# Single images at the end of a filter phase, and constants, loads and table writes moved in a hand-ordered Trainium2 kernel

## The chip, the cores and the metric

The kernel runs on one core of a Trainium2 chip. The core has a matrix engine (TensorE, PE in the profile, with PEld for its weight loads), a vector engine (VectorE, DVE), a scalar engine (ScalarE, ACT), GpSimd (POOL) and a sync engine (SyncE, SP) that mostly issues DMA transfers. All work from on-chip memory, and the products of TensorE land in PSUM banks of 128 partitions by 512 float32. Everything here is float32.

The metric is the device time of one execution in microseconds (us). A profile is one further execution under the hardware profiler; its span runs from the first to the last instruction.

## The reference, cut to what matters

Eight images of 128 channels by 32×32 pixels go through two layers. The first has attention over the 1024 pixels of an image and then a spectral transform unit (STU), the second a deformable convolution of three taps and eight experts of which two are used per pixel.

```python
# layer 0
x = x + attention(ln_c(x))                  # left as it is by the change
t = tokens(x)                               # (8, 1024, 128)
t = t + stu(ln_t(t))
# layer 1
x = image(t)
x = x + deform_conv(ln_c(x))
t = tokens(x)
t = t + experts(ln_t(t))

def stu(u):      # only one of four fractions (1, 1/2, 1/4, 1/8) of the tokens has weight 1
    U_plus[t, k]  = sum_s phi[s, k] * u[t - s]             # 16 causal filters
    U_minus[t, k] = the same with alternating signs
    return sum_k sigma[k]**.25 * (U_plus[:, k] @ Mpp[k] + U_minus[:, k] @ Mpm[k]) \
           + sum_{i<3} shift(u, i) @ Mu[i]

def deform_conv(x):   # per pixel and tap j: position = base + offset(x)
    for j in range(3):
        s = bilinear sample of x at (y, xc)                # four neighbours
        out += sigmoid(mask(x))[j] * s @ conv_w[j].T

def experts(x):       # softmax over 8, the two largest, renormalized
    return sum over the two of p * (x @ expert_w[e] + expert_b[e])
```

The fractions enter the kernel as spans of tokens: each span of an image has its own sum of the weighted matrices.

## The kernel before

**Attention.** `attention_bounded` works until about 1020 us and stores each image of the first sublayer to a DRAM buffer `x1d`. The change doesn't touch it.

**What stands between.** After a branch (line 1258), `mix_weights` works out the softmax weights of the fractions, `Spectral.__init__` builds its constants (among them `mu`, the matrices of the three lags, from four loads of `M_u` through one buffer), and `DeformAndExperts.__init__` builds the second layer's constants with some 45 small DMAs from SP. All of that is issued before the first image is prepared.

**The filter phase.** `spectral_and_second_layer` writes the order of all engines' instructions out by hand: each engine executes its instructions in the order in which this function emits them. `GROUPS` puts the images into four pairs. A group passes 16 filters, so there are 64 iterations. An iteration has four parts (parity of the token, term plus or minus), and in each part, for each image of the pair, `filter_image`: four accumulating matmuls of 512, 384, 256 and 128 columns into one of two PSUM banks (`pu`, line 1154), copied out by ACT into `us` (line 1158). Between them stand the products of the iteration before with the mixing matrices `mf` (`mix`, line 1142): per part, spans of 64, 64 and 128 tokens behind the first image and one of 256 behind the second, each over both images of the group. The first mix of a group is preceded by `start_sums`, the lags. After a group's last mix `finish` copies the sums `po` to `x2`.

`load(n + 2)`, at the end of iteration n, loads the next but one filter (`teto`, lines 1049 and 1052, three buffers) and its matrices (`mf`, three buffers). The first group builds the matrices and stores them to DRAM, later groups load them (line 1064). All of these go through SP.

**The second layer beside the filters.** `layer.image` is a generator of some 96 steps. It turns the image back to tokens, normalizes and turns again; makes eight products with the convolution weights (`p_g`, line 856), copied by ACT to `gs` (line 859); writes them as a table of four shifted slots to DRAM with 24 writes of 256 KB from SP (line 864), twelve after the fourth product and twelve after the eighth; works out positions and weights (`corners`); fetches with 24 indirect DMAs from POOL (line 894, nine buffers) and accumulates with 96 DVE operations (line 909); normalizes (`tt`), turns (`p_turn`, line 772), computes the gates (`p_l`, line 971), and applies the experts with sixteen matmuls (`p_e`, line 927) through two PSUM banks and 64 DVE operations (line 933). It ends with `p_out` (lines 944, 947) and the store.

From the second iteration of a group on, `behind` holds the two images of the group before and `spec.prepare` of the next group. After each unit of an iteration (eight units, one for each part and image) `todo` grows by `RATE`, 1.8, and as many whole steps of `behind` run. Each step's TensorE instructions therefore stand in TensorE's order between filter products, and TensorE waits there if their inputs are late.

**The tail.** Images 6 and 7 have no filters left to stand beside. They run after the last `finish`, the second one 50 steps behind the first.

Of the kernel before, what the change touches and what calls it, by code (L numbers as in the profile page):

```python
# [32 lines left out]
GROUPS = ((0, 1), (2, 3), (4, 5), (6, 7))  # L33
RATE = 1.8
STAGGER = 50
# [637 lines left out]
class DeformAndExperts:  # L673
# [4 lines left out]
    def __init__(  # L678
# [3 lines left out]
        nc = self.nc = tc.nc  # L682
        cp = ctx.enter_context(tc.tile_pool(name="d_const", bufs=1))
        self.sb = ctx.enter_context(tc.tile_pool(name="d_sb", bufs=2))
        self.ps = ctx.enter_context(tc.tile_pool(name="d_ps", bufs=banks, space=PSUM))
        self.ident, self.dram, self.out = ident, dram, out

# [8 lines left out]
        with nc.allow_non_contiguous_dma(reason="small weights"):  # L696
            for tap in range(TAPS):
                at = TAPS * C + 9 * tap
                for xy in range(2):
                    nc.sync.dma_start(  # L700
                        self.gw[:, at + 3 * xy : at + 3 * xy + 3], off_r[:, tap, xy, :]
                    )
                nc.sync.dma_start(self.gw[:, at + 6 : at + 9], mask_w[:, tap, :])
            for xy in range(2):
# [3 lines left out]
            nc.sync.dma_start(bias[:, 6:9], mask_b.partition_broadcast(P))  # L708
        nc.gpsimd.memset(self.base, 0.0)
# [8 lines left out]
        )  # L718

# [7 lines left out]
        for n in range(2):  # L727
            tab = dram.tile([TAPS, self.ROWS, 4, C], F32, name=f"tab{n}")
            for tap in range(TAPS):
                for r0 in (0, T):  # L730
                    nc.sync.dma_start(
                        tab[tap, r0 : r0 + 33].rearrange("r s c -> r (s c)"), zero
                    )
            self.tabs.append(tab)

        self.shift = [None, ident, None]
        for tap, edge in ((0, 0), (2, 31)):
# [7 lines left out]
            self.shift[tap] = s  # L745
        self.cb = cp.tile([P, C], F32, name="cb")
# [4 lines left out]
        nc.sync.dma_start(self.rb, router_b.partition_broadcast(P))  # L751
        self.ew = cp.tile([C, NE, C], F32, name="ew")
# [5 lines left out]
        for i in range(NT):  # L758
            nc.sync.dma_start(self.ebm[i * NE : (i + 1) * NE, i, :], expert_b)
        self.eidx = cp.tile([P, NT, NE], F32, name="eidx")  # L760
        nc.gpsimd.iota(self.eidx, pattern=[[0, NT], [1, NE]], base=0, channel_multiplier=0,
                       allow_small_or_imprecise_dtypes=True)

# [74 lines left out]
    def image(self, b, x2):  # L838
# [15 lines left out]
        for i in range(NT):  # L854
# [4 lines left out]
            nc.scalar.copy(gs[:, i, :], pg[:, 0:N])  # L859
            if i % 4 == 3:  # L860
                for slot, back in enumerate((0, 1, 32, 33)):
                    for tap in range(TAPS):
                        r0 = 33 - back + (i - 3) * P
                        nc.sync.dma_start(
# [3 lines left out]
            yield  # L868
        yield
# [140 lines left out]
class Spectral:  # L1010
# [4 lines left out]
    def __init__(self, ctx, tc, dram, phi_e, phi_o, M_u, M_plus, M_minus, coef, w, x1d):  # L1015
# [6 lines left out]
        self.M_plus, self.M_minus, self.coef = M_plus, M_minus, coef  # L1022
# [11 lines left out]
        self.mu = cp.tile([C, NFR, TAPS, C], F32, name="mu")  # L1034
        for f in range(NFR):
            m = self.sb.tile([C, TAPS, C], F32, tag="m_u", name="m_u")
            nc.sync.dma_start(m, M_u[f].rearrange("i d e -> d i e"))
# [46 lines left out]
    def prepare(self, group, bank):  # L1084

        nc, sb = self.nc, self.sb
        for n, b in enumerate(group["images"]):
            if n == 0:
                group["x1"], group["ur"] = [], []
                ut = group["ut"] = sb.tile([C, 2, 2, HT + 1], F32, tag="ut", name="ut")  # L1090
                nc.gpsimd.memset(ut[:, :, :, 0:1], 0.0)
            x1 = sb.tile([P, NT, C], F32, tag="x1", name="x1", bufs=2)
            nc.gpsimd.indirect_dma_start(
                out=x1.rearrange("p i c -> p (i c)"), out_offset=None,
                in_=self.x1d.rearrange("b p i c -> (b p) (i c)"),
                in_offset=bass.IndirectOffsetOnAxis(ap=self.back[:, b : b + 1], axis=0),
            )
            ur = sb.tile([P, NT, C], F32, tag="ur", name="ur", bufs=4)
            group["x1"].append(x1)
            group["ur"].append(ur)  # L1100
            yield
            yield
            yield from norm_steps(nc, sb, x1, ur, 1e-5)
            yield
            for par in range(2):
                pt = bank("p_ut")
                for i in range(4):
# [218 lines left out]
```

## Time and profile before

| what | us |
|---|---|
| device time, median of three runs | 3162.05 (3161.14 to 3165.78) |
| profiled execution, device time | 3165.82 |
| its span | 3164.1 |
| first filter product starts | 1060.87 |
| last mix ends, `finish` starts | 2926.37 |
| busy: PE, DVE, ACT, POOL | 2788.8, 1430.6, 977.2, 958.0 |

The page of the profile gives busy times and shares, then 40 equal slices of the span in which each digit is the busy share in tenths, then the costliest groups of instructions. A group's row reads: line of the kernel, engine, operation, output <- inputs by the program's names, shape and type, count | busy time in us, mean ns of one | idle time of the engine just before them, and what ended most of it. A timeline row reads: start, length, engine, line, operation, count, and in brackets the idle time before it with what ended it. Mean granted clock of TensorE is 0.951 of full speed.

### The profile page before, as it was taken

Reading aid. Unit: us, or ns where it says so; the run is one execution under the profiler, and the core shown is the slowest. Engines: PE = TensorE matmul, PEld = TensorE weight load, DVE = VectorE, ACT = ScalarE, POOL = GpSimd, SP = SyncE. Lnnn points to the kernel's source line nnn. Section 1 sums busy time; section 2 is a strip of 40 time slices with the busy share of each in tenths; the row PEclk is TensorE's granted clock in tenths of the full one; section 3 lists DMA queues with packets and bytes.
Section 4 is the critical chain, followed back from the end, with each engine's and each line's share of the span. In section 5 each row is a group of like instructions: output and inputs, shape, how many; then the busy total and the mean of one; then the engine's idle time right before and its main releaser. Section 6 shows DMA issues by size and latency. Waiting matters only on the chain.

```text
span 3164.1 us, 45167 instructions
## 1 busy us (share of the span) xinstructions
PE 2788.8 (88%) x18888; PEld 1709.7 (54%) x18888; DVE 1430.6 (45%) x2908; ACT 977.2 (31%) x1152; POOL 958.0 (30%) x876
## 2 busy tenths in 40 slices
PE   5898998998997699999999999989899989899154
PEld 2454454454553466666566566656566656566022
DVE  1677778777787320000243531153332144241477
ACT  2665656666664121111212112211212211211100
POOL 1666666666775210000210300120200030200331
PEclk9999999999999799999999999999999999999566
DMA  0000000000000422221520611331611241510541
GB/s 24 8 8 8 15 3 14 15 2 8 9 8 14 119 67 61 72 62 40 154 73 30 204 40 60 119 108 34 197 36 54 87 140 47 170 57 14 159 133 40
DMA packets 176724, 198.76 MB, mean 63 GB/s; under 512 B 17205, under 2 KB 135157, under 8 KB 176513
## 3 DMA queue, kind: packets, MB, share of 16 engines
q1 hardware_dynamic: 160000, 141.26, 15.0%
q0 software_dynamic: 16512, 54.54, 5.8%
q8 instruction: 150, 2.46, 0.3%
q14 instruction: 62, 0.50, 0.0%
HBM read 127.83 MB, written 67.92 MB: 62 GB/s over the span
## 4 chain that ended last, share of the span: by engine, by line
PE 80%; ACT 7%; DVE 7%; issue 3%; DMA 1%; POOL 1%; SPq 1%; another core or an unknown queue 1%; POOLq 0%; DVEq 0%; ACTq 0%
PE pu L1154 35%; PE po L1142 16%; PE s L509 9%; ACT e L514 6%; PE av L561 4%; PE p_e L927 3%; PE z L530 3%; DVE x L909 2%; PE rb L544 2%; PE p_g L856 1%; PE pk L478 1%; DVE x L933 1%; PE pq L464 1%; DVE e L551 1%
## 5 line engine op out<-in xcount | busy, mean ns | idle before, releaser
L1154 PE MATMUL pu<-teto,ur 128*128 128x512 f32 (+3 forms) x4096 | 1206.0, 438 | 53.5 <-issue 42.3
L1154 PEld LDWEIGHTS pu<-teto,ur 128*128 128x128 f32 x4096 | 779.3, 192 | 606.2 <-issue 417.4
L1158 ACT COPY us<-pu 128x512 f32<-128x512 f32 x512 | 299.6, 585 | 1351.2 <-PE pu L1154 1199.0
L523 POOL TENSOR_TENSOR t<-e 128x1024 f32<-128x1024 f32 x256 | 607.0, 2372 | 356.3 <-ACT e L514 354.1
L551 DVE TENSOR_TENSOR e<-e,rb 128x2048 f32<-128x2048 f32 x256 | 569.6, 2281 | 119.3 <-PE rb L544 119.3
L514 ACT ACTIVATE e<-s 128x2048 f32<-128x2048 f32 x256 | 480.8, 1878 | 277.3 <-PE s L509 255.0
L1142 PE MATMUL po<-us,mf 128*128 128x128 f32 (+2 forms) x2048 | 530.6, 382 | 0.0
L509 PE MATMUL s<-q,k 32*128 32x256 f32 x4096 | 301.1, 409 | 75.9 <-ACT e L514 75.7
L894 POOL DMA_INDIRECT g<-tab,cn_idx x192 | 184.9, 963 | 438.6 <-DMA teto<-in_phi_e 240.8
L643 POOL TENSOR_SCALAR rs_v<-rs_v 128x8 f32<-128x8 f32 x24 | 5.9, 246 | 1020.3 <-DVE rs_b L641 1020.3
L509 PEld LDWEIGHTS s<-q,k 32*128 32x128 f32 x4096 | 188.9, 188 | 203.0 <-ACT e L514 165.8
L561 PE MATMUL av<-e,vt 128*32 128x256 f32 x4096 | 277.6, 389 | 4.0 <-DVE e L551 2.7
L1142 PEld LDWEIGHTS po<-us,mf 128*128 128x128 f32 x2048 | 272.0, 193 | 4.1 <-issue 3.9
L909 DVE SCALAR_TENSOR_TENSOR x<-g,w,x 128x128 f32<-128x128 f32 x704 | 248.0, 352 | 51.3 <-DVE x L909 24.2
L933 DVE SCALAR_TENSOR_TENSOR x<-p_e,gates,x 128x128 f32<-128x128 f32 x512 | 177.1, 350 | 171.2 <-PE p_e L927 154.6
L561 PEld LDWEIGHTS av<-e,vt 128*32 128x32 f32 x4096 | 107.9, 110 | 136.4 <-issue 76.3
L537 DVE RECIPROCAL r<-z 128x256 f32<-128x256 f32 x64 | 112.4, 1757 | 98.4 <-PE z L530 98.1
L927 PE MATMUL p_e<-ew,tc 128*128 128x512 f32 x256 | 137.5, 650 | 15.8 <-DVE x L933 12.7
L1076 DVE TENSOR_SCALAR mf<-both,coef 128x256 f32<-128x256 f32 x16 | 5.6, 353 | 290.8 <-PE po L1142 246.2
L530 PE MATMUL z<-t,group 128*32 128x256 f32 x2048 | 135.4, 382 | 0.0
L878 DVE TENSOR_TENSOR om<-p_om,base 128x72 f32<-128x72 f32 x8 | 1.9, 231 | 240.3 <-PE p_om L873 240.3
L1174 DVE COPY x<-po 128x512 f32<-128x512 f32 x8 | 5.5, 692 | 221.3 <-ACT x L1174 221.3
(199 smaller groups left out, 1607.5 us busy)
## 6 DMA issues: line engine op xcount, KB each, us to landing
tab<-gs SPq DMA_DIRECT2D x192, 256.0 KB
mf<-mfd SPq DMA_DIRECT2D x48, 512.0 KB
teto<-in_phi_o SPq DMA_DIRECT2D x64, 256.5 KB
teto<-in_phi_e SPq DMA_DIRECT2D x64, 256.0 KB
mfd<-mf SPq DMA_DIRECT2D x16, 512.0 KB
xc<-in_x SPq DMA_DIRECT2D x8, 512.0 KB
x1d<-xt SPq DMA_DIRECT2D x8, 512.0 KB
mp<-in_M_plus SPq DMA_DIRECT2D x16, 256.0 KB
```

The source lines that it names most:

```text
L509: nc.tensor.matmul(s[:, j, c, :], img["k"][rows, hg, 2 * r + c, :], q[rows, qc * QU : (qc + 1) * QU], start=True, stop=True,)
L514: nc.scalar.activation(e.rearrange("p j c q -> p (j c q)"), s.rearrange("p j c q -> p (j c q)"), AF.Exp, scale=float(HD) ** -0.5,)
L523: nc.gpsimd.tensor_add(t, e[:, :, 0, :], e[:, :, 1, :])
L530: nc.tensor.matmul(un["z"][32 * j : 32 * j + 32, 0:QU], group, un["t", r][:, j, :], start=(r == 0), stop=(r == 3), skip_group_check=True,)
L551: nc.vector.tensor_tensor(e, e, un["rb"].unsqueeze(2).to_broadcast([P, NH, 2, QU]), ALU.mult)
L561: nc.tensor.matmul(qrt["av"][32 * j : 32 * j + 32, 0:QU], img["v"][:, 2 * r + c, P * hg + 32 * j : P * hg + 32 * j + 32], un["e", r][:, j, ...
L909: nc.vector.scalar_tensor_tensor(x3[:, i, :], g[:, k * C : (k + 1) * C], w[:, i, tap, k : k + 1], (tok if tap + k == 0 else x3)[:, i, :], ...
L927: nc.tensor.matmul(pe, tc[:, i * P : (i + 1) * P], self.ew[:, grp * 4 : grp * 4 + 4, :].rearrange("d e c -> d (e c)"), start=True, stop=True,)
L933: nc.vector.scalar_tensor_tensor(x3[:, i, :], pe[:, k * C : (k + 1) * C], gate[:, i, grp * 4 + k : grp * 4 + k + 1], x3[:, i, :], ALU.mult ...
L1142: self.nc.tensor.matmul(out, lhsT, rhs, start=bank not in group["opened"], stop=last, skip_group_check=True)
L1154: nc.tensor.matmul(pu[:, i * P : HT], group["ur"][n][:, src * 4 + i, :], flt[:, 0 : HT - i * P], start=(i == 0), stop=(i == 3),)
L1158: nc.scalar.copy(us[:, n, :], pu)
```

## The change

`GROUPS` becomes `((0, 1), (2, 3), (4, 5), (6,), (7,))`: images 6 and 7 pass the filters one after the other, so that image 6 goes through the second layer while image 7 is filtered, and only image 7 is left for the tail. There are then 80 iterations. `RATE` is 2.0 for pairs and 2.7 for single images, and steps run only after a unit with a filter product. The preparation of image 7 stands behind the first image of its predecessor pair in `behind`.

The second layer's constants become a generator `setup`, the first entry of `behind`. At the head, two filters are loaded and image 0 and 1 prepared before `mix_weights` (`weigh`), the first matrices, `lags` (the `M_u` loads) and the second matrices. `load_filter(n + 2)` moves from the end to the start of iteration n; the matrices stay at the end. Table writes yield after each group of three, and the image of the tail (`alone`) issues every other one from ACT. `prepare` becomes one generator per image, with the same instructions.

```diff
-GROUPS = ((0, 1), (2, 3), (4, 5), (6, 7))
-RATE = 1.8
-STAGGER = 50
+GROUPS = ((0, 1), (2, 3), (4, 5), (6,), (7,))
+RATE = (2.0, 2.7)
...
+    def setup(self):
+        nc, cp, ident, dram = self.nc, self.cp, self.ident, self.dram
...
                 nc.sync.dma_start(self.gw[:, at + 6 : at + 9], mask_w[:, tap, :])
+                yield
...
-    def image(self, b, x2):
+    def image(self, b, x2, alone):
...
             nc.scalar.copy(gs[:, i, :], pg[:, 0:N])
+            yield
             if i % 4 == 3:
                 for slot, back in enumerate((0, 1, 32, 33)):
                     for tap in range(TAPS):
+                        queue = nc.scalar if alone and (slot + tap) % 2 else nc.sync
                         r0 = 33 - back + (i - 3) * P
-                        nc.sync.dma_start(
+                        queue.dma_start(
...
-            yield
-        yield
+                    yield
...
+    def lags(self, w):
+        nc = self.nc
         for f in range(NFR):
             m = self.sb.tile([C, TAPS, C], F32, tag="m_u", name="m_u")
-            nc.sync.dma_start(m, M_u[f].rearrange("i d e -> d i e"))
+            nc.sync.dma_start(m, self.M_u[f].rearrange("i d e -> d i e"))
...
-def spectral_and_second_layer(tc, spec, layer):
+def spectral_and_second_layer(tc, spec, layer, weigh):
     groups = [{"images": im} for im in GROUPS]
-    for _ in spec.prepare(groups[0], layer.bank):
+    work = [(g, k) for g in range(len(groups)) for k in range(NF)]
+    filters = {n: spec.load_filter(n) for n in range(2)}
+    first, *others = spec.prepare(groups[0], layer.bank)
+    for run in (first, *others):
+        for _ in range(7):
+            next(run)
+    for _ in chain(first, *others):
         pass
-    work = [(g, k) for g in range(len(groups)) for k in range(NF)]
-    loaded = {}
-
-    def load(n):
-        if n < len(work):
-            g, k = work[n]
-            loaded[n] = spec.load_filter(k), spec.load_matrices(k, g == 0)
-
-    behind, done, todo = iter(()), 0, 0.0
-    load(0)
-    load(1)
+    w = weigh()
+    matrices = {0: spec.load_matrices(0, True)}
+    spec.lags(w)
+    matrices[1] = spec.load_matrices(1, True)
+
+    behind = deque([layer.setup()])
+    starts = {}
+    todo = 0.0
+
+    def advance(steps):
+        nonlocal todo
+        todo += steps
+        while todo >= 1:
+            todo -= 1
+            while behind and next(behind[0], behind) is behind:
+                behind.popleft()
+
     before = None
     for n in range(len(work) + 1):
         now = work[n] if n < len(work) else None
         if now is not None and now[1] == 1:
             g = now[0]
-            tasks = [layer.image(b, groups[g - 1]["x2"][:, m]) for m, b in
-                     enumerate(groups[g - 1]["images"])] if g else []
+            if g:
+                for m, b in enumerate(groups[g - 1]["images"]):
+                    behind.append(layer.image(b, groups[g - 1]["x2"][:, m], False))
             if g + 1 < len(groups):
-                tasks.append(spec.prepare(groups[g + 1], layer.bank))
-            behind = chain(*tasks)
+                starts[g + 1] = chain(*spec.prepare(groups[g + 1], layer.bank))
+                behind.insert(1 if len(groups[g]["images"]) == 1 else len(behind), starts[g + 1])
+        if now is not None and now[1] == 0 and now[0]:
+            for _ in starts[now[0]]:
+                pass
+        if n + 2 < len(work):
+            filters[n + 2] = spec.load_filter(work[n + 2][1])
...
             for m in range(2):
-                if now is not None and m < len(group["images"]):
-                    spec.filter_image(group, m, par, term, loaded[n][0], us)
+                unit = now is not None and m < len(group["images"])
+                if unit:
+                    spec.filter_image(group, m, par, term, filters[n], us)
...
-                todo += RATE
-                while todo >= 1:
-                    todo -= 1
-                    next(behind, None)
+                if unit:
+                    advance(RATE[2 - len(group["images"])])
         if before is not None and before[1] == NF - 1:
-            for _ in behind:
-                pass
             spec.finish(groups[before[0]])
-        load(n + 2)
+        if n + 2 < len(work):
+            matrices[n + 2] = spec.load_matrices(work[n + 2][1], work[n + 2][0] == 0)
         kept, before = sums, now
-    runs = [layer.image(b, groups[-1]["x2"][:, m]) for m, b in enumerate(groups[-1]["images"])]
-    alive, step = [], 0
-    while runs or alive:
-        if runs and step % STAGGER == 0:
-            alive.append(runs.pop(0))
-        alive = [r for r in alive if next(r, r) is not r]
-        step += 1
+    while behind:
+        advance(1)
+    for m, b in enumerate(groups[-1]["images"]):
+        for _ in layer.image(b, groups[-1]["x2"][:, m], True):
+            pass
```

## The prediction

> **What bounds the kernel now.** I read the page first, its busy shares and its slices.
>
> ```profile
> PE 2788.8 (88%) x18888; PEld 1709.7 (54%) x18888; DVE 1430.6 (45%) x2908; ACT 977.2 (31%) x1152; POOL 958.0 (30%) x876
> ...
> PE   5898998998997699999999999989899989899154
> ...
> PEclk9999999999999799999999999999999999999566
> ```
>
> One slice is 79 us. TensorE is full from slice 14 to 37, the filter phase, and nearly idle in the last three, where images 6 and 7 go through the second layer with no filter left to cover them. From the first filter product (1060.87) to the end of the last mix (2926.37) is 1865.5 us; from there to the end 237.7. Next, the stretches of that tail (columns: length, busy time and instructions of PE, PEld, DVE, ACT, POOL, then granted clock, DMA share, GB/s):
>
> ```profile
> 2926.00:2944.00 18.00, 8.61 (x28) 4.48 (x27) 7.03 (x29) 5.58 (x10) 5.05 (x14) 0.72 0.00 0
> 2944.00:2968.00 24.00, 4.35 (x21) 2.37 (x20) 4.18 (x24) 3.31 (x7) 0.00 (x0) 0.66 0.90 262
> 2972.00:3014.00 42.00, 0.00 (x0) 0.00 (x0) 34.77 (x110) 0.00 (x0) 20.53 (x22) 0.50 0.49 142
> 3014.00:3112.00 98.00, 49.54 (x119) 22.57 (x119) 73.53 (x245) 8.07 (x17) 30.66 (x52) 0.64 0.46 134
> 3112.00:3164.00 52.00, 29.01 (x89) 14.28 (x89) 31.62 (x110) 2.86 (x6) 2.81 (x14) 0.76 0.03 11
> ```
>
> Image 6 turns and normalizes (18 us), writes its table (24, DMA nearly full, all engines idle), gathers and accumulates (42, DVE); then both images share 98 us, and image 7 alone needs the last 52. So the tail is one chain of latencies per image, little overlapped.
>
> Then the groups inside the filter phase, with their waits, and the timeline of TensorE at one of them:
>
> ```profile
> L1154 PE MATMUL pu<-teto,ur 128*128 128x512 f32 (+3 forms) x4096 | 1206.0, 438 | 53.5 <-issue 42.3
> ```
>
> ```profile
> 1572.50 2.32 PE L1154 MATMUL pu<-teto,ur 128*128 128x512 f32 x8
> 1574.65 1.04 PE L1142 MATMUL po<-us,mf 128*128 128x128 f32 x6
> 1582.53 4.36 PE L1154 MATMUL pu<-teto,ur 128*128 128x512 f32 x8 [6.83 <-issue]
> 1586.72 1.02 PE L1142 MATMUL po<-us,mf 128*128 128x512 f32 x2
> 1589.77 1.15 PE L1154 MATMUL pu<-teto,ur 128*128 128x512 f32 x1 [2.03 <-ACT us L1158]
> ```
>
> The waits of the phase add up to 7 to 11 us for each of six images, all within that image's gathers, and the product behind a long wait takes 4.36 us in place of 2.32. ACT shows why TensorE stood still: its copies, which free the two product banks, come late.
>
> ```profile
> 1568.86 0.58 ACT L1158 COPY us<-pu 128x512 f32<-128x512 f32 x1 [2.49 <-issue]
> 1581.89 0.58 ACT L1158 COPY us<-pu 128x512 f32<-128x512 f32 x1 [12.45 <-issue]
> ```
>
> What held ACT 12.45 us the trace doesn't name. No filter load was under way in 1575 to 1583 (only the gathers' queue moves bytes), and the filters used there had been issued at 1558 to 1561.
>
> My account of the 1865.5: 512 filter products at 2.157 are 1104.4; 256 mix units at 1.74 are 445.4; four start sums at 14.9, 59.6; turning the inputs, 11.2. What is left, 244.9, over six images is **40.8 us per image**: some 28 of its own matmuls, 12.5 of waits and half-speed products after them.
>
> **What the skill says.** "DMA: Bandwidth & Descriptors", section "Issuing engines are not separate DMA queues": another issuing engine saves only issue time. The trace agrees that issue isn't the limit: in 2956 to 2960 the table writes keep DMA at 0.99, 282 GB/s, from SP alone. "TensorE: Matmul & The Clock Gate", section "LDWEIGHTS (loading the stationary operand)": a weight load goes by columns, 107 ns for 128. The trace agrees: sixteen products with only eight moving columns take 1.70 us (p_l), 106 ns each, weights bound. Same page, "Part 1: The HAM clock gate (the "warmup" mystery)": after idling the array runs at about half rate; 4.36 against 2.32 above agrees.
>
> **The change part by part**, against the profiled execution's span, 3164.1 (device time 3165.82).
>
> *Head, −1.* Before: last x1d store issued 1020.26, image 0's gather 1030.04 behind ~45 constant loads on SP, first product 1060.87, start sums 1080.33, lag products with mu from 1082.3. After: nothing but the filters' four loads stands between the branch (1025.1) and the gather, so the first product comes at 1060.87 − 4.7 − 2.4 ≈ 1053.7 (the second image's gather no longer waits either). But the mixing weights now follow the preparation (two 1.28 us ACT table loads, 3.3 us of DVE), and M_u's four loads through one buffer (4.33 us a step) start after the first mixing matrix, at about 1063: mu is whole at 1080.5. The lag products then start at 1080.5 against 1082.3. With ±4 for the hand-made order. The constants made in 23 steps lie under the filters of group 0, where DVE, ACT and SP are idle (DVE is busy 45 of 439 us): 0. Uncovered they would be the 7 us already counted.
>
> *Filters loaded further ahead, 0.* They were issued an iteration or more ahead of use, and the waits above have no filter load under way. They now pass the iteration's table writes on SP (21.5 us for 24); nothing waited there. The matrix loads stay behind those writes, and in the single phases two iterations, 2×4×(2.157+1.07) = 25.8 us, are their cover: thin, but the writes come in two lots of twelve. If the filters were the cause, up to 53.5 + 18 come back: rival C.
>
> *Table writes by step and over two queues, 0.* 6.29 MB at 284 GB/s are 22 us however issued. Finer steps (96 to 103 per image) keep the writes behind the same copies; SP waits alone. In image 7 six writes stand on ACT ahead of copies 4 to 7; at SP's 0.9 each (21.53 by 24) that is 5.4 us, plus 4 copies, inside the 11 that the first half's bytes take.
>
> *Narrow mixing, +25.6.* A pair mixes in 0.88 (128, 128 and 256 columns, two passes) and 0.86 (512). A single image has 64, 64, 128, then 256. At 106 ns as the floor of a pass: 2×(0.106+0.106+0.11) = 0.64, and 0.43. Two singles cost 2×1.07 = 2.14 against 1.74: +0.40, times 64. Start sums 8.2 each against 14.9 a pair: +1.5. One more group boundary: +0.7.
>
> *Image 6 under image 7's filters, +40.8*, by the account above.
>
> *Denser steps in the single phases, +25.* A step there stands for (2.157+1.07)/2.7 = 1.195 us of filter work; before (2.157+0.87)/1.8 = 1.68. From an image's first table write to its second turn TensorE has 55 steps: 55×1.195 = 65.7, plus 3.5 of its own matmuls and 12.5 of waits, 81.7 us. DVE needs 36.5 until accumulation starts, 40 for it (39.2 to 40.9 in the trace) and 8.6 to normalize: 85.6. Before, DVE had room:
>
> ```profile
> 1615.93 2.14 DVE L665 TENSOR_SCALAR tt<-x,mv,rs_y 128x128 f32<-128x128 f32 x8 [3.55 <-POOL rs_y L648]
> ...
> 1633.94 0.60 PE L772 MATMUL p_turn<-ident,tt 128*128 128x128 f32 x4
> ```
>
> 15.9 us from the end of the first to the start of the second; at single rate this is gone, and TensorE waits about 4, plus 1 at half rate, in order, with all filters queued behind it. Then sixteen expert products come up to three in a bundle on two banks, each freed by four DVE operations at 0.35: the third waits about 0.83, 3.3 an image. In all 8.3, three images (4, 5 and 6). The pairs' steps go from 1.68 to 1.515, which leaves 99 us: 0.
>
> *Tail, −100.7.* One image: 45.6 from the last filter to its first gathered data (2926.4 to 2971.95), 40 of accumulation, 52.3 for the rest (image 7, 3111.8 to 3164.1), −0.8 for finer writes: 137 against 237.7. Image 6 finishes four to five filter units before the last, so nothing spills.
>
> Sum: −1 + 25.6 + 1.5 + 0.7 + 40.8 + 25 − 100.7 = **−8.1**. Span 3156.0, device time 3157.7. The profiled execution is at the upper end of the three runs, 3.8 above the median; the difference goes on the median, 3162.05 − 8.1 ≈ 3154.
>
> **Rivals.** A, no extra wait: TensorE lags its schedule in the single phases because the 12.5 us of waits fall elsewhere, so DVE keeps its room: −8.1 − 25 = −33, 3129. For it: 4 us is a narrow miss on a sum of 85.6. Against: the expert stage needs 64×0.35 = 22.4 us of DVE in 18×1.195 = 21.5.
>
> B, slower: the single phases become bound by the second layer's DVE and gather chain. Point of decision: extra waits above 33/3 = 11 us an image. Accumulation then need only stretch by 3 us from my 40 (in gathers' stretches DVE's operations already take 0.7 to 1.4 instead of 0.387), as TensorE's waits feed back: a late copy, a late step, then half rate. At 18 us an image the change is at +22, 3184; up to +40.
>
> C, the filter loads do cause the waits of 53.5 and the slow products after them: about −8 − 72 = −80, 3082. Against: nothing on SP's queue in those gaps.
>
> D, the edit does less than it says: the step count spills image 6 beyond the last filter. By its count it has 323 steps in 334.8, so no; were it to, the loss is counted in B.
>
> **How the numbers follow.** 0.2% is 6.3 us, about what a measurement here can tell from none. The forecast has 0.45, own range −20 to +4 (head ±4, waits ±8): 0.26 faster, 0.19 the same. A 0.20, faster. B 0.28: 0.03 the same, 0.25 slower. C 0.03, faster; something unforeseen, 0.04, slower. Faster 0.49, same 0.22, slower 0.29. To leave out 2 in 10, the range drops C and what lies over 7 us below A (low 3122, together 0.06), and B above +24 with the unforeseen (high 3186, 0.14).
>
> **What would show it.** Right: the last mix ends near 3019 (2926.4 − 1 + 93.6), the tail after it is 137; mix forms with 64 columns at 106 ns a pass; waits at the second turn in the single phases of some 4 us, none in the pairs; the gathers' waits with late ACT copies still there. A shows no wait at the second turn; B waits above 11 us an image there or at the expert products; C no late copies. Wrong altogether if the head gains 7 (mu early), the tail is not 137, or a table write, now ahead of others in a queue, holds up a filter.

## The result

The changed kernel takes 3192.03 us (median of four runs) against 3161.6 for the kernel before: a ratio of 1.0100, with a 95% interval of 1.008 to 1.0121. It is 30 us slower. The forecast was 8 us faster, and its range ended at 3186. The profiled execution took 3191.81 us, its span is 3190.1, 26.0 more than before.

From the page of the profile after, the rows that answer to those of before:

```profile
PE 2811.8 (88%) x19448; PEld 1772.2 (56%) x19448; DVE 1430.8 (45%) x2910; ACT 974.7 (31%) x1152; POOL 960.3 (30%) x877
...
L1179 PE MATMUL pu<-teto,ur 128*128 128x512 f32 (+3 forms) x4096 | 1211.2, 439 | 78.5 <-issue 51.8
...
L1167 PE MATMUL po<-us,mf 128*128 128x128 f32 (+3 forms) x2560 | 570.6, 351 | 6.3 <-issue 6.3
```

TensorE's busy time rises by only 23 us, but its waits at the filter products rise from 53.5 to 78.5, and 6.3 at the mixing are new. To place them I cut both traces at the copies that end a group's sums. The windows of the kernel before and then of the kernel after (start and end, length, busy time and instructions of PE, PEld, DVE, ACT, POOL, granted clock, DMA share, GB/s):

```profile
1060.70:1483.20 422.50, 422.50 (x1714) 277.06 (x1714) 43.91 (x118) 82.50 (x141) 47.47 (x61) 1.00 0.24 67
1483.20:1971.10 487.90, 471.00 (x1903) 304.97 (x1903) 162.50 (x570) 97.97 (x173) 69.50 (x133) 0.98 0.30 91
1971.10:2458.50 487.40, 468.35 (x1904) 303.69 (x1903) 163.02 (x570) 96.69 (x172) 69.52 (x133) 0.98 0.30 91
2458.50:2926.40 467.90, 448.01 (x1806) 289.24 (x1804) 151.48 (x516) 89.70 (x161) 62.05 (x104) 0.98 0.29 87
2926.40:3164.00 237.60, 91.18 (x254) 43.70 (x254) 151.19 (x516) 19.79 (x40) 61.93 (x104) 0.65 0.38 111
```

```profile
1057.10:1497.30 440.20, 426.03 (x1715) 278.86 (x1714) 47.02 (x138) 85.71 (x147) 49.71 (x78) 0.98 0.24 68
1497.30:1992.80 495.50, 469.97 (x1903) 304.84 (x1902) 162.93 (x570) 96.60 (x172) 69.78 (x133) 0.98 0.30 90
1992.80:2476.50 483.70, 458.98 (x1855) 297.08 (x1855) 157.19 (x543) 93.22 (x166) 65.98 (x119) 0.98 0.30 91
2476.50:2764.50 288.00, 262.58 (x1270) 190.73 (x1270) 111.20 (x393) 55.38 (x100) 61.21 (x103) 0.95 0.48 147
2764.50:3055.60 291.10, 265.93 (x1272) 189.62 (x1270) 121.65 (x410) 47.41 (x88) 36.08 (x68) 0.96 0.32 99
3055.60:3190.00 134.40, 41.94 (x127) 21.48 (x127) 75.66 (x259) 10.12 (x21) 31.55 (x52) 0.66 0.34 98
```

The first filter product comes 3.5 us earlier, but the first group ends 14.1 later, with the same work (1714 and 1715 TensorE instructions). The second group takes 7.6 more. The third takes 3.7 less, and should take 10 less: four filter products of the next group (4×2.157 = 8.6) and 1.4 us of preparation moved out of it. The two single phases, images 6 and 7 in turn, take 579.1 against the last pair's 467.9, the tail 134.4 against 237.6.

| stretch | forecast, us | measured, us | off by |
|---|---|---|---|
| head and first group | −1 | +14.1 | +15.1 |
| second and third group, with what moved out put back | 0 | +13.9 | +13.9 |
| single phases, without the four products (8.6), with the preparation (1.4) that moved in | +95.0 | +102.6 | +7.6 |
| tail | −100.7 | −103.2 | −2.5 |
| sum, with the 1.4 of preparation counted out of the third group | −8.1 | +26.0 | +34.1 |

Nearly all of the first group's loss is one wait. The timelines of TensorE, of POOL and of SP's issues there, in the kernel after (start, length, engine, line, operation, and in brackets the idle time ahead of it):

```profile
1133.54 2.08 PE L1133 MATMUL p_ut<-flip,ur 128*128 128x128 f32 x8 [13.22 <-DVE ur L665]
1135.41 4.17 PE L1179 MATMUL pu<-teto,ur 128*128 128x512 f32 x8
```

```profile
1113.65 1.27 POOL L1093 TENSOR_TENSOR both<-mp,mm 128x512 f32<-128x512 f32 x1 [24.95 <-DMA mm<-in_M_minus]
1116.55 1.08 POOL L1118 DMA_INDIRECT x<-x1d,back  x1 [0.16 <-issue]
```

```profile
1095.34 10.36 SPq L744 DMA_DIRECT2D tab<-zero  x12
1108.89 0.51 SPq L1091 DMA_DIRECT2D mm<-in_M_minus  x1
```

Read from the bottom. SP issues the constants, among them twelve writes that clear the tables and hold it for 10.36 us. Behind them stand the loads of the third iteration's mixing matrices. POOL, idle for 24.95 us by then, forms their sum when they land, and the gather of image 2's input is queued behind that sum on POOL. After it the normalization of this input stands behind the next matrices too, on POOL and DVE. The turn of image 2's input, which stands early in TensorE's order, waits 13.22 us with all filter products behind it, and the first of these takes 4.17 us in place of 2.32. These two are 15.1 us; before, TensorE had no idle time in its first group (422.50 busy of 422.50).

The gathers' waits are of the old kind, with longer gaps of ACT (timelines of ACT and TensorE of the kernel after, in image 4's gathers):

```profile
2569.90 0.59 ACT L1183 COPY us<-pu 128x512 f32<-128x512 f32 x1 [17.75 <-remote]
```

```profile
2552.29 2.32 PE L1179 MATMUL pu<-teto,ur 128*128 128x512 f32 x8
...
2570.54 4.63 PE L1179 MATMUL pu<-teto,ur 128*128 128x512 f32 x8 [11.57 <-ACT us L1183]
```

Per image they were 8.9 us (53.5 over six) and are 12.1 (78.5 + 6.3 over seven). No second turn (the turn of the normalized sums, `p_turn` from `tt`) waits anywhere in the filter phase.

### The profile page after: what moved, and what is told of

Same layout as the page of the kernel before. It is cut to its first block, busy times and chain, and to the rows that moved or that the text cites. A ratio compares the mean times of both kernels' runs of the same rounds, so it can differ in the third digit from the quotient of the medians.

```text
span 3190.1 us, 46453 instructions
## 1 busy us (share of the span) xinstructions
PE 2811.8 (88%) x19448; PEld 1772.2 (56%) x19448; DVE 1430.8 (45%) x2910; ACT 974.7 (31%) x1152; POOL 960.3 (30%) x877
## 4 chain that ended last, share of the span: by engine, by line
PE 77%; ACT 8%; DVE 6%; issue 4%; another core or an unknown queue 2%; DMA 2%; POOL 1%; SPq 0%; ACTq 0%; POOLq 0%; DVEq 0%
PE pu L1179 33%; PE po L1167 15%; PE s L509 9%; ACT e L514 6%; PE av L561 4%; PE p_e L946 3%; PE z L530 3%; PE rb L544 2%; PE p_g L874 1%; PE pk L478 1%; DVE x L952 1%; DVE x L928 1%; PE pq L464 1%; DVE e L551 1%
## 5 line engine op out<-in xcount | busy, mean ns | idle before, releaser
L1179 PE MATMUL pu<-teto,ur 128*128 128x512 f32 (+3 forms) x4096 | 1211.2, 439 | 78.5 <-issue 51.8
L1167 PE MATMUL po<-us,mf 128*128 128x128 f32 (+3 forms) x2560 | 570.6, 351 | 6.3 <-issue 6.3
L1167 PEld LDWEIGHTS po<-us,mf 128*128 128x128 f32 x2560 | 338.5, 194 | 20.6 <-issue 20.1
L946 PE MATMUL p_e<-ew,tc 128*128 128x512 f32 x256 | 125.9, 604 | 13.2 <-DVE x L952 13.2
L1093 POOL TENSOR_TENSOR both<-mp,mm 128x512 f32<-128x512 f32 x16 | 20.3, 1266 | 290.5 <-DMA mm<-in_M_minus 290.5
```

Of the source, the lines that this page charges most:

```text
L946: nc.tensor.matmul(pe, tc[:, i * P : (i + 1) * P], self.ew[:, grp * 4 : grp * 4 + 4, :].rearrange("d e c -> d (e c)"), start=True, stop=True,)
L1167: self.nc.tensor.matmul(out, lhsT, rhs, start=bank not in group["opened"], stop=last, skip_group_check=True)
L1179: nc.tensor.matmul(pu[:, i * P : HT], group["ur"][n][:, src * 4 + i, :], flt[:, 0 : HT - i * P], start=(i == 0), stop=(i == 3),)
```

## The experiments

The runs were made in several sets, each on one chip, and these differ: in three sets the kernel before takes 3079 to 3080 us, in the others 3159 to 3162. Every ratio is to the kernel before in the same set. No chip is on record for more than one set, so what follows can't tell a chip from the moment of its set; I say "chip" for both. I call the slower ones "chips with late copies", for the reason shown next.

### Does the late ACT copy belong to the kernel?

The kernel before and the kernel after were profiled again, unedited.

> The kernel before, profiled on the chip of these runs. The four runs above were made on a chip on which it takes 3079, not 3162, and their traces have no wait of TensorE in the gathers. Theory (the late ACT copies belong to the first chip, not to the kernel): on a chip where it takes about 3079 its filter products show no waits and each pair's phase takes 441 to 463 us; on one where it takes about 3162 the waits of 16 to 19 us a pair are there. Rival (the earlier kernels lack the waits because of what was edited in them): at 3079 the waits of the kernel before are there all the same, and the difference lies in the attention or the tail.

> The changed kernel beside it. If the chip is one without the waits: the first group's wait of 13 us at the turn of image 2, pairs at 462.6 and 452.2, then waits of about 10 us at the second turns in the single phases and of 12 us at the start sums of image 7, in all 3111 to 3117, a ratio of 1.010 to 1.013. If it is one with the waits: 3192, ratio 1.010, no waits at the second turns. A rival, that moving the filter loads is what costs: below 3105 here, since the kernel with those loads moved back took 3117.

The chip was one with late copies: 3161.43 (one run) and 3191.76, ratio 1.0097 (1.0071 to 1.0122). TensorE's waits of the kernel before are there again, 51.9 us at the filter products. In the kernel after they are 79.2 and 5.3 at the mixing, 12.1 an image. On the three other chips no filter product waits for a copy in the gathers, in any kernel. The timelines of TensorE, ACT and POOL of one such kernel (the run with the constants moved, below) in image 0's gathers:

```profile
1571.66 2.32 PE L1179 MATMUL pu<-teto,ur 128*128 128x512 f32 x8
```

```profile
1574.02 0.59 ACT L1183 COPY us<-pu 128x512 f32<-128x512 f32 x1 [2.40 <-PE pu L1179]
```

```profile
1576.24 0.95 POOL L913 DMA_INDIRECT g<-tab,cn_idx  x1 [0.30 <-DVE x L928]
```

POOL issues as densely as ever, 0.30 us between two gathers, and ACT copies on time: the product ends at 1573.98, its copy begins at 1574.02. So the late copies go with the chip, and dense issue of gathers isn't enough to cause them.

The traces do show what ACT stands in. Its waits ahead of the copies in the filter phase of the kernel after, then before (total, number, longest), and DVE's in its accumulations before:

```profile
ACT us L1183 <- remote: 146.0, 16, 17.7
ACT us L1158 <- remote: 93.5, 16, 14.0
DVE x L909 <- DVE x L909: 18.7, 28, 1.5
```

"Remote" means that a semaphore event ended the wait and that the profile finds no instruction of this core that ended just then. The eight traces from chips with late copies have 93.5 to 163.1 us of such waits of ACT, the twelve others none; nor do DVE's accumulations wait for DVE itself in those. In the example above the product of 2552.29 ended by its record at 2554.61 and its copy began at 2569.90; the semaphore that ACT waits for there is one that only TensorE's instructions raise. So ACT wasn't busy: it waited for word of a product that the trace has as finished 15.3 us earlier. Whether the word was late, or the product ended later than its record (ends of products are modelled), and why only on some chips, stays open.

### The constants in steps

```diff
-    behind = deque([layer.setup()])
+    behind = deque()
...
+            if g == 0:
+                behind.append(layer.setup())
```

The two new lines stand after the preparation of the next group has been put into the list.

> The changed kernel with one move: the generator of the second layer's constants stands behind the preparation of the next group in the list, not ahead of it. Theory (constants' DMAs on SP hold up the loads of the third filter's matrices, these hold POOL, and with it the gather for image 2): the wait of 13.2 us at the turn of image 2's input and the half-speed product behind it go, 3192 - 15 = 3177 us, the first group's finish 15 us earlier. Rival (the constants' work costs its time wherever it stands among the filters): the wait turns up elsewhere in the first group and the time stays within 5 us of 3192. Rival that it hurts only at the head: the same 3177.

3100.41, ratio 1.0070 (1.0053 to 1.0086), on a chip without late copies. The wait of 13.2 us is down to 1.7, and the first group takes 426.2 us, not 440.2. The changed kernel itself never ran on such a chip, so the gain is taken from pairs of kernels: the first group takes 439.4 to 440.2 us in all six traces with the constants ahead and 424.5 to 426.2 in all eleven with them behind. The theory holds: 14 us, for the place on SP and not for the work, which still lies under the first group. In device time the three pairs of kernels that differ in this and little else, all shown below, give 11 to 14 us.

### Single images against a pair

```diff
-GROUPS = ((0, 1), (2, 3), (4, 5), (6,), (7,))
+GROUPS = ((0, 1), (2, 3), (4, 5), (6, 7))
```

The tail is that of before, with its lead of 50 steps.

> The changed kernel with images 6 and 7 as a pair again, staggered by 50 steps in the tail as before, and no table writes from ACT. Measured in the traces, single images lengthened the last phase by 102.6 us and shortened the tail by 103.2. Theory (these cancel, and what made the change slow lies in the phases of the pairs and the first group): 3192 within 6 us. Rival (single images are the loss): 3165 to 3180. Rival (they gain, as forecast): 3198 or more.

3087.99, ratio 1.0033 (1.0021 to 1.0045), on the same chip. Against the runs with single images there (1.0070 even without the constants' 14 us) the pair is clearly better, as the rival had it. "They cancel" was read from traces of the other chips, where this kernel never ran. The waits of the run with the constants moved show why (TensorE, from the end of the third group to the end of the filters):

```profile
PE p_turn L790 <- DVE tt L665: 19.7, 2, 11.2
PE po L1167 <- issue: 11.9, 1, 11.9
PE p_e L946 <- DVE x L952: 7.5, 9, 0.8
PE p_out L963 <- DVE x L952: 2.5, 3, 0.8
```

Without late copies TensorE does reach the second turns before DVE, as forecast: 11.2 and 8.5 us in images 4 and 6. In image 5 TensorE has been held earlier, at the start sums of image 7 (timelines of DVE and TensorE of the same run):

```profile
2675.48 4.23 DVE L928 SCALAR_TENSOR_TENSOR x<-g,w,x 128x128 f32<-128x128 f32 x11
...
2680.49 0.42 DVE L1199 COPY x<-po 128x256 f32<-128x256 f32 x1 [0.45 <-ACT x L1199]
```

```profile
2681.02 1.19 PE L1167 MATMUL po<-flip,x 128*128 128x128 f32 x4 [11.89 <-issue]
```

The boundary between the two single groups falls into image 5's accumulation. Two of the copies that empty the sums stand on DVE behind it, some 12 us late, and the next sums need those banks: they start 0.11 us after the second of these copies, the one shown, ends. I had not seen this wait coming.

### The constants moved, and the pair kept

```diff
-GROUPS = ((0, 1), (2, 3), (4, 5), (6,), (7,))
+GROUPS = ((0, 1), (2, 3), (4, 5), (6, 7))
...
-    behind = deque([layer.setup()])
+    behind = deque()
```

Both edits above in one kernel.

> The changed kernel with two parts undone, images 6 and 7 a pair with the staggered tail and the constants behind the preparation; 2.0 steps a unit, filters loaded ahead, table writes spread. On a chip without the late ACT copies: 3088 (the pair alone undone) less 14 for the constants, 3074, 0.998 of the kernel before. On one with them: the single images and the tail cancel there, so 3178 within 6 us, with 21 to 31 us of waits in each of the second to fourth groups.

3076.06, ratio 0.9988 (0.9981 to 0.9995), without late copies: 4 us faster than the kernel before. Beside the run with single images and the same constants (1.0070) this prices single images on such chips at 0.0082×3080 = 25 us, within some 6. Its last phases are

```profile
2404.50:2846.30 441.80, 440.95 (x1806) 286.60 (x1804) 151.64 (x516) 89.61 (x161) 62.38 (x104) 1.00 0.30 92
2846.30:3071.00 224.70, 88.06 (x254) 42.51 (x254) 151.04 (x516) 19.88 (x40) 63.12 (x104) 0.67 0.39 117
```

With 462.6 for the group ahead that is 1129.1 us; single images take 452.1 + 272.9 + 296.3 + 133.7 = 1155.0. By this account the 43.9 us of waits (19.7 + 11.9 + 7.5 + 2.5, and 2.3 at the gates) turn a gain of some 18 into a loss of 26; no run took the waits away to show it.

### Filter loads back at the end

```diff
-        if n + 2 < len(work):
-            filters[n + 2] = spec.load_filter(work[n + 2][1])
         sums = {}
...
         if n + 2 < len(work):
+            filters[n + 2] = spec.load_filter(work[n + 2][1])
             matrices[n + 2] = spec.load_matrices(...)
```

> The changed kernel with the filter loads back at the end of an iteration, ahead of the matrices. Theory (loading earlier is worth nothing): 3192 within 6 us, and the waits inside the gathers stay at 10 to 14 us an image. Rival (filter loads that now run at another time than before are what made the waits grow from 9 to 12 us an image in the pairs' phases): about 20 us less, 3170. Rival (the earlier loads do help): 3200 or more, with waits of TensorE on filter loads behind table writes.

> The changed kernel with the constants moved behind and the filter loads back at the end of an iteration. On a chip with the late copies: if the new place of the filter loads made the waits in the pairs' phases grow from 15 to 19 us to 21 to 31 a pair, they shrink to 15 to 19 and the time is 3165 or less; if it has no part in it, 3178 within 6, waits of 21 to 31. On a chip without: 3100 to 3106.

Both ran without late copies: 1.0119 (1.0102 to 1.0136) and, with the constants moved, 1.0082 (1.0065 to 1.0099), which is 3.7 us over the same kernel with the loads ahead, within the uncertainty of the two. One filter product waits 1.6 to 2.0 us for a load. Loading ahead is worth a few us at most there, and nothing measurable with pairs, in the last two kernels under "Denser steps".

### Gathers paced

```diff
-                g = sb.tile([P, 4 * C], F32, tag="g", name="g", bufs=9)
+                g = sb.tile([P, 4 * C], F32, tag="g", name="g", bufs=4)
```

The loop issues a gather three ahead of its use, in place of the three gathers of a tile two tiles ahead.

> The changed kernel with the gathers of an image issued at most three ahead of their use, through four buffers in place of nine. Theory (ACT's late copies come with POOL issuing gathers back to back, 0.30 us between two): paced by DVE at about 1.54 us a gather, the waits of TensorE at the filter products (78.5 us, and 6.3 at the mixing) and the half-speed products after them mostly go, 60 to 90 us, so 3102 to 3132 us. Rival (the transfers' load, 6.3 MB an image, is what slows ACT): the same bytes move at 20 percent less rate, the waits shrink by a fifth, 3175 to 3190. Rival (accumulation becomes bound by the latency of a gather): 3192 or more, with waits at the second turn.

> The kernel before with its gathers issued at most three ahead of use through four buffers. On a chip with the late ACT copies (the kernel before takes about 3160): if gathers issued back to back on POOL hold ACT, pacing them takes away the 7 to 11 us of waits an image and the half-speed products, up to 12.5 for six images, 75 us: 3085 to 3110. If the load of the gathers is what holds it, less than 15 us are gained. On a chip without the late copies: within 10 us of the kernel before, since pacing lengthens only the tail's two accumulations.

> As pairs_later with the gathers at most three ahead through four buffers. On a chip with the late copies: if gathers issued back to back hold ACT, 3178 less 60 to 90; if not, within 15 us of pairs_later. On a chip without: as pairs_later within 5, since pacing cost the kernel before nothing there (3079.05 against 3079.2).

None met a chip with late copies, so the theory of dense issue was not tested there. The first took 3125.61 us, within the range that the theory gave, and that is chance: the kernel before takes 3079 on that chip. Without late copies pacing does next to nothing where pairs are filtered: 1.0002 (0.9994 to 1.0011) for the kernel before, 0.9996 (0.9988 to 1.0005) with the constants moved and the pair, 3 us over the same kernel unpaced. With single images it costs: 1.0149 (1.0132 to 1.0165), against 1.0119 on the same chip for the kernel of the section above, which also has the constants ahead. The waits at the second turns are 29.7 us there, not 19.7, so it looks as if TensorE lost at the turn what DVE lost in the accumulation.

### Easing the single phases

In these kernels, and in those of the next section, the constants stand behind.

```diff
-                copy = self.nc.vector.tensor_copy if par else self.nc.scalar.copy
+                copy = self.nc.vector.tensor_copy if par and n_img > 1 else self.nc.scalar.copy
```

> The changed kernel with the constants behind the preparation, and with the four copies that end a single image's sums all on ACT (of before: two on ACT, two on DVE, in turn). Theory (the DVE copy stands behind some thirty accumulations of image 5, and TensorE waits for it with the start sums of image 7): the wait of 11.9 us goes, but DVE is as late as before, so about 10 of it come back at the second turn of image 5: 3100 less 0 to 5 on a chip without waits in the gathers. Rival (only the copy is late): 3088. Where the chip has the waits in the gathers: 3177, nothing gained by the copies.

With late copies: 3178.49, 1.0054 (1.0031 to 1.0078). The first group takes 425.4 us against 439.7 of the changed kernel on that chip, and the difference in time, 13.3 us, is the constants'. The copies gain nothing there.

```diff
                             gs[:, i - 3 : i + 1, tap * C : (tap + 1) * C],
                         )
-                    yield
...
+        for _ in range(8):
+            yield
         tt = sb.tile([P, NT, C], F32, tag="ht", name="tt")
```

> As finish_act, with the eight steps of an image that separate its table writes taken out and eight empty steps put behind its accumulation, so that the count stays 103 and DVE has 8 times 1.2 us more until the second turn. Theory (in the single phases TensorE reaches the second turn before DVE): the waits at the second turns, about 20 to 30 us with the half-speed products behind them, mostly go: 3065 to 3078, that is 0.995 to 1.000 of the kernel before on a chip without waits in the gathers. Rival (the narrow mixing and the experts' waits are the larger part of what single images cost): 3090 or more. Where the chip has the waits in the gathers: 3170 to 3177.

> The kernel with the constants moved behind, the copies on ACT and eight steps moved, its gathers paced in the same way. On a chip with the late copies, if back-to-back issue is the cause: 3181 less 60 to 90, 3090 to 3120; if not, 3165 or more. On a chip without them: 3065 to 3085 if the moved steps cover DVE's lateness, 3095 or more if they don't.

Both keep the copies on ACT. 1.0070 (1.0044 to 1.0096) with late copies, and, paced, 1.0072 (1.0055 to 1.0089) without. The wait at the start sums is gone in the latter, and the second turns wait 27.3 us all the same. The edit was ill-made: the steps that I took out also lie between the first table write and the turn, so their number there stays 55.

```diff
+                        filler = starts[g + 1] if g + 1 < len(groups) else range(9)
...
+        for _ in filler:
+            yield
         tt = sb.tile([P, NT, C], F32, tag="ht", name="tt")
```

The steps of the preparation of image 7 run inside image 4, nine empty ones inside image 6; the eight of the edit above are not in it.

> As finish_act (constants behind the preparation, the single images' copies on ACT), single images kept, with other work put between accumulation and second turn: in image 4 the fourteen steps that prepare image 7, in image 6 nine empty steps, 17 and 11 us for DVE to catch up. On a chip without the late ACT copies: the waits of 11.2 and 8.5 us at these turns and of 11.9 at the start sums go, with some 6 of half-speed products: 3100 less 20 to 38, 3062 to 3080, 0.995 to 1.000 of the kernel before. If the steps don't reach DVE's lateness, as in the kernel with eight steps moved: 3095 or more. On a chip with the late copies: 3178 within 6.

> The changed kernel again, for its trace beside one of the edited ones on the same chip. On a chip without the late copies, where it has not run yet: 3100 (constants moved behind) plus 14, 3111 to 3117, 1.010 to 1.013 of the kernel before; first group with 13 us of wait, pairs at 462.6 and 452.2, second turns waiting 9 to 12 us twice, start sums of image 7 for 12. On one with them: 3192, 1.010, waits of 21 to 31 us in the pairs' phases a third time.

Both met late copies: 1.0056 (1.0037 to 1.0075) and 1.0107 (1.0090 to 1.0123). There are no waits at the turns there to remove, so this way of easing single images remains untried where it could help. The changed kernel shows its 12.0 us of waits an image a third time.

### Denser steps

```diff
-RATE = (2.0, 2.7)
+RATE = (1.8, 2.7)
```

> The changed kernel with the constants moved behind and 1.8 in place of 2.0 steps a unit in the pairs' phases, as before; some ten steps of image 6 then spill past the last filter, 5 to 10 us. On a chip with the late copies: if the denser steps made the waits in the pairs' phases grow, the waits of the second and third group fall to 15 to 19 us each; if not, they stay at 21 to 31. The time is 3178 + 5 to 10, less up to 20. On a chip without: 3105 to 3115.

> As pairs_later with 1.8 steps a unit and 96 steps an image, as before (no step of its own for a slot of the table). On a chip without the late copies: 3074 within 4. On one with them: if denser steps made the waits in the gathers grow, they fall back to 15 to 19 us a group and the time to 3155 to 3160; if not, 3178 and 21 to 31 us a group.

> As pairs_later_18, and the filter loads back at the end of an iteration: what is left of the change is the order of the head. On a chip without the late copies: 3076 within 4. On one with them: 3156 within 5 and 15 to 19 us of waits a group in any case; beside pairs_later_18 it tells whether the place of the filter loads is what made them grow (then 15 to 25 us faster than that kernel) or has no part (the same).

None met late copies. With single images 1.0037 (1.0025 to 1.0050), 10 us better than at 2.0, which I had not expected. The two single phases take 561.1 us, not 569.2, and their waits are 8.1 + 7.3 at the turns and 10.3 at the start sums, not 11.2, 8.5 and 11.9, which is 5.9 of it. With the pair, and the steps of before, 1.0004 (0.9996 to 1.0013), and with the filter loads at the end too 1.0004 (0.9997 to 1.0011): what is left there is the head's order and the constants among the filters, and they are worth nothing measurable. The tail takes 232.7 us with the coarse steps of before and 224.7 with the fine ones, so of the changed kernel's parts only the finer steps, which shorten the lead of image 6 over image 7, showed a gain here.

What made the gathers' waits grow from 8.9 and 8.7 us an image (53.5 and 51.9 over six, the two traces of the kernel before) to 11.3 to 12.8 (six traces of changed kernels, with late copies) is therefore not settled. It isn't the spread table writes, which the eased kernel hasn't (12.5), and not the constants. The denser steps and the place of the filter loads remain.

## Why the prediction was wrong

The forecast was −8.1 us and the span grew by 26.0. The terms that failed are the constants' "0", the denser pair steps' "0" and, with errors that partly cancel, the single phases.

**The constants, "0".** This step failed first: 15.1 of the 34.1 us. I named DVE, ACT and SP as idle under group 0 and counted busy time, but SP issues in order. The step list put its loads ahead of the matrices of the third filter, POOL and DVE wait for these in order too, and image 2's preparation is behind them. Undoing it gave 14 us back in the first group.

**The pairs' denser steps, "0".** Right at the second turn, where no pair waits in any trace. But I took the gathers' waits as a constant of the kernel, 12.5 us an image with the slow products. In the profiled execution the four images of the two pair groups wait 48.6 us where they waited 34.4 before, about the 13.9. No edit was shown to be the cause, so what made this term fail stays open.

**The single phases, "+25".** The terms were off in both directions, and the phases came out 7.6 us longer. At the second turn I had 15 us and found 0: where copies are late TensorE falls behind, and DVE keeps some room (1.3 us in image 4, some 10 in images 5 and 6, where it had 15.9), as rival A said. On the chips without late copies the mechanism is there with 19.7. (DVE's sum was also added wrongly: 36.5, 40 and 8.6 are 85.1, not 85.6.) The gathers' waits of the three images are 36.1 us where three times 8.9 had been in the account, +9.4. The experts' waits, gates included, are 12.3 us (forecast 9.9):

```profile
2997.98 1.10 PE L946 MATMUL p_e<-ew,tc 128*128 128x512 f32 x2 [0.83 <-DVE x L952]
```

**Narrow mixing, "+25.6".** Right, but 4 short:

```profile
3037.93 2.32 PE L1179 MATMUL pu<-teto,ur 128*128 128x512 f32 x8
3040.09 1.27 PE L1167 MATMUL po<-us,mf 128*128 128x64 f32 x8
3041.19 2.32 PE L1179 MATMUL pu<-teto,ur 128*128 128x512 f32 x8
```

A unit of filter and mixing takes 3.26 us where I had 3.227; over 128 units that is 4.2 us. The eight mixing products take 1.10 us of it, where the floor of 106 ns a pass had given 1.07, so the floor stands. (It is a spacing: the record of a single weight load is about 192 ns long, so the loads overlap.) With −15, +9.4, +2.4 and +4.2, 6.6 of the 7.6 us are unassigned; the slow products behind the longer waits are the likely place, which I did not separate.

**Head, tail, filter loads, table writes.** The first filter product starts at 1057.1 (forecast 1053.7) and the lag products at 1079.7 (forecast 1080.5). Before, the trace has these at 1060.66 and 1081.95, a little ahead of the 1060.87 and 1082.3 that I worked from. The tail is 134.4 (forecast 137). The filter loads are worth nothing that can be told from none; what the split of the last image's writes over two queues is worth was not measured by itself, and the tail leaves 2.5 us for it.

**The rivals.** B named single phases bound by DVE as the way to a slower kernel, with 3184 for it. The sign came from elsewhere on the chips of the forecast. On the others it came from B's place: 43.9 us over three images are 14.6 an image, above B's 11. A was right that no second turn waits on the chips of the forecast, and wrong in its time. C fell: with the filters loaded further ahead the waits grew. So did D: image 6 ends at 3037.7, the last filter product at 3050.0.

## What to carry to other kernels

When instructions are put into idle time, follow each queue they enter to the next thing behind them, and that thing's consumers, until one stands on the bound engine: busy shares say nothing of it. A step placed by count into an in-order engine's stream is safe only while its producer has slack; write that slack down per phase, since a denser phase spends it. And ask what a phase boundary interrupts on every engine: a copy of 0.42 us cost 12 because it stood behind another task's work.

## What the runs showed of the hardware

Two things I had not expected. The same program differs by 2.6% between chips (3079 to 3080 against 3159 to 3162), the same in all runs of a set. Of the 90 us between the two traces compared here, 77 lie in the three phases that hold gathers beside filters (487.9, 487.4 and 467.9 in the kernel before, against 462.6, 462.0 and 441.8 in the same kernel paced, on a chip of the other kind), where ACT's copies on the slower chips come up to 17.75 us after the one before, after waits that end on an event which the profile gives to no instruction. And an edit can be worth different amounts on the two kinds: single images cost 25 us on the one by a pair of runs, and on the other, by the windows of one trace alone, their longer phases (+102.6) and shorter tail (−103.2) cancel. A trace from one chip priced them wrongly for another.
